# The B product of eight states as pairs in two row groups of the array, and the C product and sum of eight others in four column groups

## Chip, cores and metric

One core of one Trainium2 chip. The metric is the time of one execution on the device in microseconds; lower is better. Before the change three runs took 13143.59, 13146.60 and 13146.84 us, median 13146.6. All data is float32.

## What is computed

Two layers with a residual each. Layer 0 is a two-dimensional recurrence over a 64 x 64 image of 128 channels, 16 images. Layer 1, which the change touches, normalises its input in groups of channels and runs a selective state-space scan (Mamba) over the 4096 tokens of an image, once forwards and once backwards, with the same weights. Cut to layer 1, for one direction, with 256 inner channels d and 16 states s:

```python
xz = x @ in_w.T
xc, z = jnp.split(xz, 2, axis=-1)
xt = lax.conv_general_dilated(xt, conv_w[:, None, :], ..., feature_group_count=D_INNER)
xc = jax.nn.silu(jnp.transpose(xt, (0, 2, 1)))
dbl = xc @ x_w.T
dt, Bm, Cm = jnp.split(dbl, [DT_RANK, DT_RANK + D_STATE], axis=-1)
dt = jax.nn.softplus(dt @ dt_w.T + dt_b)
dA = jnp.exp(dt[..., None] * A)
dBx = dt[..., None] * Bm[:, :, None, :] * xc[..., None]
def step(h, inp):
    dA_t, dBx_t, C_t = inp
    h = dA_t * h + dBx_t
    y = jnp.einsum('bds,bs->bd', h, C_t)
    return (h, y)
y = jnp.swapaxes(ys, 0, 1) + xc * D
y = y * jax.nn.silu(z)
return y @ out_w.T
```

So for each of 16 states there is a decay exp(dt A), a drive dt x B (B is one number per token and state), a scan over the tokens, a product with C (again one number per token and state), and a sum over the states.

## The kernel before

Layer 0 comes first and takes about 1,560 us of the profiled execution. Layer 1 then makes 256 passes: 16 images, in each eight chunks of 512 tokens forwards and the same eight backwards. Channels lie on the 128 partitions in NH = 2 halves h, tokens along the free dimension; NB = 4 blocks j of 128 tokens make a chunk.

A pass does the following. PE convolves as eight products with shifted input (conv), ACT applies silu, PE makes dt, B and C (xproj, which already runs as two groups of 64 columns of the array), ACT copies them out, and they go to DRAM as 32 rows of 512 (rows). dtproj and softplus give dt; POOL multiplies dt and xc (times, giving dtx); PE turns dtx to have tokens on the partitions (turn), and ACT copies it (turn_take, giving dtxt). Then the states. For each, ACT makes the decay of the two halves (decay), DVE scans each half (scan, L1230), the last column is kept for the next chunk (keep, into carry), the state is multiplied by C (out_of; the row of C was spread over the partitions by a DMA of 256 KB, cr), and PE adds the turned product into the PSUM tile py (sums, eight turning matmuls). After all states, skip adds xc D, and finish takes py out; a forwards pass puts it in DRAM, a backwards pass adds it back (again), multiplies by the gate, turns it (back), projects it and stores it.

A string of letters, KINDS, says for each of the 16 states how its drive and its output are made:

- P: POOL multiplies dtx by the row of B spread over the partitions (drive, L1185); the decay lies in PSUM.
- M and T: ACT multiplies the turned dtx by B, a scalar per partition there, in four instructions (drive_turned, L1192); PE turns it back into PSUM (drive_back, L1218).
- N and U: PE turns back and multiplies at once, as a product with a diagonal matrix of B (drive_back, L1209). The diagonals dg are put together in DRAM by a DMA of single words onto a zeroed matrix (scatter, L1202), and loaded (spread).
- T and U scan in place in PSUM, and DVE makes their product with C (L1258); for all other letters POOL makes it (L1256).

Forwards passes have five M, four P, four N, two T, one U; backwards passes six M, five P, two N, two T, one U. In all that is 4.5 drives and 13 products with C on POOL a pass.

The order of all work on every engine is fixed when the program is built: order_of_issue lists the operations with costs (COST), priorities (URGENCY) and ring buffers (RINGS), and simulate places them, engine by engine, in an order. PSUM has eight banks: two for py, six handed out one by one, of which at most two at a time for "misc" (conv, xproj, dtproj, turn, gate, back, project) and at most five for decays and drives. The DMAs named here are all issued by SP, in order, and a DMA that must wait holds up those behind it. Softplus, silu and exp need different tables on ACT, so silu and softplus of passes ahead are gathered in a "session", with no decay between.

Of the kernel before, what the change touches and what calls it, by code (L numbers as in the profile page):

```python
# [14 lines left out]
P = 128  # L15
# [21 lines left out]
KINDS = ("MPNTMNPMUNPTMNPM", "MPMTPNMPTMPUMNPM")  # L37

RINGS = {
    "bank": 6, "py": 1, "das": 4, "dbx": 4, "dbt": 3, "dg": 3, "hst": 4, "hc": 5,  # L40
    "br": 4, "cr": 5, "xc": 2, "dt": 2, "dtx": 2, "dtxt": 2, "dbl": 2, "bt": 2, "z": 1, "y": 1,
    "yt": 1, "xr": 1, "xl": 1, "yo": 1, "yl": 1,
# [3 lines left out]
    "conv": 0.865, "gate": 0.87, "silu": 0.62, "softplus": 0.65, "gate_take": 0.6, "dtproj": 0.95,  # L46
    "xproj": 1.0, "xproj_take": 0.4, "bturn": 0.25, "bturn_take": 0.15, "times": 2.34,
    "turn": 0.47, "turn_take": 0.47, "decay": 0.62, "drive": 2.34, "drive_turned": 1.6,
    "drive_back": 0.44, "drive_back_diag": 0.88, "scan": 1.18,
    "keep_turned": 0.13, "keep": 0.6, "out_turned": 0.6, "out": 2.34, "sums": 0.88, "skip": 0.44,  # L50
# [7 lines left out]
LIMIT = {"misc": 2, "bank": 5}  # L58
AHEAD = 3
# [5 lines left out]
        {(0, 0): -27.9, (0, 1): -55.24, (0, 2): -37.14, (0, 3): -26.5, (1, 0): -25.66, (1, 1): -31.09,  # L65
         (1, 2): -28.23, (1, 3): -24.41},
        {(0, 0): -34.48, (0, 1): -62.91, (0, 2): -27.86, (0, 3): -25.86, (1, 0): -33.52, (1, 1): -26.55,
         (1, 2): -34.72, (1, 3): -27.13},
    ),
    "xproj": (  # L70
        {(): -7.14},
        {(): 5},
    ),
    "xproj_take": (
        {(): -0.87},
        {(): -6.61},
    ),
    "rows": (
        {(): 6.65},
        {(): 22.72},  # L80
    ),
    "bturn": (
        {(): -69.81},
        {(): -79.06},
    ),
    "bturn_take": (
        {(): -11.43},
        {(): -18.91},
    ),
    "dtproj": (  # L90
        {(0,): -63.21, (1,): -27.76},
        {(0,): -42.3, (1,): -15.88},
    ),
    "times": (
        {(): -134.9},
        {(): -152.1},
    ),
    "turn": (
        {(0,): -117.7, (1,): -95.41},
        {(0,): -92.29, (1,): -73.14},  # L100
    ),
    "turn_take": (
        {(0,): -12.62, (1,): -21.64},
        {(0,): -15.32, (1,): -17.24},
    ),
    "decay": (
        {(0, 0): 1.62, (0, 1): -12.81, (1, 0): -13.82, (1, 1): -8.37, (2, 0): 9.59, (2, 1): 7.54,
         (3, 0): -3.93, (3, 1): -3.12, (4, 0): -25.4, (4, 1): 2.96, (5, 0): 16.41, (5, 1): 14.98,
         (6, 0): -14.89, (6, 1): -7.22, (7, 0): 17.61, (7, 1): 6.71, (8, 0): -49.21, (8, 1): -31.38,
         (9, 0): 30.2, (9, 1): 28.66, (10, 0): -15.29, (10, 1): -11.14, (11, 0): -39.1, (11, 1): -52.04,  # L110
         (12, 0): 11.3, (12, 1): 12.04, (13, 0): -4.72, (13, 1): -9.28, (14, 0): -8.46, (14, 1): 9.15,
         (15, 0): 6.51, (15, 1): 10.38},
        {(0, 0): -11.72, (0, 1): -13.95, (1, 0): -23.83, (1, 1): -23.36, (2, 0): 5.39, (2, 1): 3.65,
         (3, 0): -27.89, (3, 1): -33.87, (4, 0): -17.63, (4, 1): -10.29, (5, 0): -5.06, (5, 1): 8.98,
         (6, 0): -5.94, (6, 1): 4.1, (7, 0): 5.44, (7, 1): 12.02, (8, 0): -73.78, (8, 1): -77.71,
         (9, 0): 21.8, (9, 1): 10.89, (10, 0): -3.99, (10, 1): -15.28, (11, 0): -27.37, (11, 1): -37.65,
         (12, 0): 21.39, (12, 1): 9.09, (13, 0): -2.78, (13, 1): -3.97, (14, 0): -1.99, (14, 1): 19.81,
         (15, 0): 11.27, (15, 1): 19.92},
    ),
    "spread": (  # L120
        {("c", 0): -1.78, ("c", 1): -117.27, ("b", 1): -23.09, ("c", 2): -80.12, ("d", 2): -40.37,
         ("c", 3): -18.07, ("c", 4): -0.55, ("c", 5): -99.41, ("d", 5): -52.16, ("c", 6): -133.17,
         ("b", 6): -13.49, ("c", 7): -18.83, ("c", 8): -39.5, ("d", 8): 9.08, ("c", 9): -42.09,
         ("d", 9): -26.61, ("c", 10): -81.5, ("b", 10): -14.43, ("c", 11): -35.04, ("c", 12): -76.62,
         ("c", 13): -69.54, ("d", 13): 21.06, ("c", 14): -21.91, ("b", 14): -26.12, ("c", 15): -95.57},
        {("c", 0): -14.51, ("c", 1): -135.28, ("b", 1): -22.37, ("c", 2): -75.2, ("c", 3): 26.76,
         ("c", 4): -11.36, ("b", 4): -10.82, ("c", 5): -37.95, ("d", 5): 9.47, ("c", 6): -122.31,
         ("c", 7): -91.31, ("b", 7): -6.34, ("c", 8): -1.04, ("c", 9): -15.62, ("c", 10): -118.12,
         ("b", 10): -20.57, ("c", 11): -6.63, ("d", 11): 42.13, ("c", 12): -104.85, ("c", 13): -62.16,
         ("d", 13): 36.52, ("c", 14): -56.98, ("b", 14): -28.81, ("c", 15): -80.03},  # L130
    ),
    "drive_turned": (
        {(0,): 4.39, (3,): 8.43, (4,): -6.7, (7,): -0.75, (11,): 7.02, (12,): -6.99, (15,): -17.26},
        {(0,): -1.81, (2,): -23.9, (3,): -35.33, (6,): -11.17, (8,): -20.91, (9,): -60.49, (12,): 7.71,
         (15,): 0.83},
    ),
    "drive_back": (
        {(0, 0): 3.71, (0, 1): 1.89, (2, 0): -5.19, (2, 1): -6.19, (3, 0): -4.81, (3, 1): 0.01,
         (4, 0): -2.71, (4, 1): 0.38, (5, 0): -18.47, (5, 1): 5.45, (7, 0): 9.18, (7, 1): 10, (8, 0): 9.85,
         (8, 1): 10.09, (9, 0): 10.62, (9, 1): 10.75, (11, 0): 3.53, (11, 1): 12.69, (12, 0): 4.21,  # L140
         (12, 1): 14.29, (13, 0): 12.99, (13, 1): 14.53, (15, 0): 16.89, (15, 1): 17.89},
        {(0, 0): -2.14, (0, 1): -4.49, (2, 0): -12.32, (2, 1): 4.91, (3, 0): -12.93, (3, 1): -0.55,
         (5, 0): -12.51, (5, 1): -4.37, (6, 0): -3.25, (6, 1): -2.4, (8, 0): 4.69, (8, 1): -1.16,
         (9, 0): 7.45, (9, 1): 9.75, (11, 0): 10.55, (11, 1): 10.75, (12, 0): 11.8, (12, 1): 14.97,
         (13, 0): 16.19, (13, 1): 16.9, (15, 0): 18.18, (15, 1): 10.8},
    ),
    "scan": (
        {(0, 0): 70.25, (0, 1): 59.47, (1, 0): 8.22, (1, 1): 9.32, (2, 0): -9.21, (2, 1): -2.84,
         (3, 0): 51.28, (3, 1): 75.32, (4, 0): 55.73, (4, 1): 59.47, (5, 0): 137.02, (5, 1): 138.28,
         (6, 0): 27.09, (6, 1): 15.69, (7, 0): 32.24, (7, 1): 37.07, (8, 0): 94.24, (8, 1): 108.17,  # L150
         (9, 0): 0.44, (9, 1): 28.19, (10, 0): 73.98, (10, 1): 59.24, (11, 0): 106.87, (11, 1): 94.54,
         (12, 0): -14.38, (12, 1): 5.54, (13, 0): 148.93, (13, 1): 161.13, (14, 0): 96.47, (14, 1): 100.3,
         (15, 0): 3.43, (15, 1): -30.56},
# [38 lines left out]
    ),  # L192
    "skip": (
        {(0,): -68.58, (1,): -75.02, (2,): -55.13, (3,): -52.01},
        {(0,): -75.1, (1,): -65.37, (2,): -44.94, (3,): -60.81},
    ),
    "finish": (
        {(): -74.82},
# [1203 lines left out]
```

## Time and profile before

| what | value |
|---|---|
| median of three runs | 13146.6 us |
| span of the profiled execution | 13233.8 us |
| starts of dtx, first and last of 256 | 1581.8 and 13159.4 us |
| scans, mean | 1261 ns, 32 a pass |
| products on POOL, mean | 2374 ns, 18.5 a pass |
| decays on ACT, mean | 713 ns into SBUF, 683 ns into PSUM |
| table loads on ACT, mean | 1283 ns, about 3 a pass |
| DMA of layer 1 | 0.63 to 0.65 of 16 engines busy, 165 GB/s |

The profile's columns: an engine's busy time counts overlapping instructions once, the mean is that of single instructions. PE's matmuls follow each other before the one ahead has ended, so a mean of 274 ns goes with a start every 109. "PEld" is the loading of the stationary matrix. A float32 product is two records of PE, a turning matmul one. In a group's line, behind the bar, stand its busy time, the mean duration in ns, and the idle time of the engine just before these instructions with what ended most of it. A line of the timeline gives the start in us, the duration of a merged run of equal instructions, engine, line and count.

### The profile page before, as it was taken

What the parts mean: (1) busy time and instruction counts of PE and PEld (TensorE: products, weight loads), DVE (VectorE), ACT (ScalarE), POOL (GpSimd) and SP (SyncE); (2) the same over time, 40 slices, a digit from 0 to 9 for tenths busy, and PEclk for the clock granted to TensorE, in tenths of its full rate; (3) what the DMA queues carried; (4) which work ended last, traced back from release to release, by engine and by line L of the source; (5) the groups of instructions that cost most, each with busy time, mean ns of one, the idle gap of its engine ahead of it and who ended that gap; (6) DMA issues with size and microseconds to landing.
All of it is one profiled execution on the core that took longest, in us unless ns stands there. A gap on an engine that the chain in (4) does not pass through costs nothing. (4 is left out here: it accounts for less than half of the span.)

```text
span 13233.8 us, 263820 instructions
## 1 busy us (share of the span) xinstructions
PE 12901.2 (97%) x91444; PEld 10833.0 (82%) x91444; DVE 12067.0 (91%) x14353; ACT 11513.4 (87%) x21184; POOL 11261.4 (85%) x4996
## 2 busy tenths in 40 slices
PE   8999999999999999999999999999999999999999
PEld 7666788888888888888888888888888888888887
DVE  6776699999999999999999999999999999999998
ACT  3444599999999999999999999999999999999998
POOL 0111299999999999999999999999999999999998
PEclk8999999999999999999999999999999999999999
DMA  4222265656666666656566666666665656666665
GB/s 143 54 57 54 63 172 158 172 156 172 161 167 165 164 165 160 172 158 172 158 170 161 166 165 163 166 159 172 158 173 160 169 162 168 164 163 166 163 166 145
DMA packets 2777751, 2025.28 MB, mean 153 GB/s; under 512 B 1584848, under 2 KB 1930464, under 8 KB 2776416
## 3 DMA queue, kind: packets, MB, share of 16 engines
q1 hardware_dynamic: 2698464, 1973.16, 57.5%
q10 hardware_dynamic: 77952, 35.24, 1.1%
q8 instruction: 725, 11.88, 0.4%
q14 instruction: 610, 5.00, 0.1%
HBM read 1849.24 MB, written 157.02 MB: 152 GB/s over the span
## 5 line engine op out<-in xcount | busy, mean ns | idle before, releaser
L1256 POOL TENSOR_TENSOR hc<-hst,cr 128x1024 f32<-128x1024 f32 x3328 | 7800.2, 2374 | 327.7 <-DVE hst L1230 243.2
L1230 DVE TENSOR_TENSOR_SCAN hst<-das,carry,hps 128x512 f32<-128x512 f32 x3808 | 4668.3, 1261 | 190.3 <-PE hps L1218 93.8
L1265 PE MATMUL py<-ident,hc 128*128 128x128 f32 x32768 | 4150.1, 274 | 57.2 <-POOL hc L1256 56.5
L1265 PEld LDWEIGHTS py<-ident,hc 128*128 128x128 f32 x32768 | 3676.6, 141 | 451.7 <-issue 272.5
L1180 ACT ACTIVATE das<-dt,A_log_sb 128x512 f32<-128x512 f32 x5888 | 3875.9, 713 | 121.5 <-DVE hst L1230 79.2
L1192 ACT ACTIVATE dbt<-dtxt,bt 128x256 f32<-128x256 f32 x7680 | 3231.7, 498 | 159.0 <-PE hps L1218 146.9
L1185 POOL TENSOR_TENSOR dbx<-dtx,br 128x1024 f32<-128x1024 f32 x1152 | 2724.6, 2378 | 10.1
L1230 DVE TENSOR_TENSOR_SCAN hst<-da,carry,dbx 128x512 f32<-128x512 f32 x2016 | 2468.8, 1260 | 31.7 <-ACT da L1180 30.0
L1218 PE MATMUL hps<-ident,dbt 128*128 128x128 f32 x15360 | 2264.2, 274 | 133.8 <-DVE hc L1258 109.3
L1209 PE MATMUL hps<-dg,dtxt 128*128 128x128 f32 x16384 | 2175.2, 277 | 38.7 <-DVE hst L1230 20.2
L1218 PEld LDWEIGHTS hps<-ident,dbt 128*128 128x128 f32 x15360 | 1783.9, 141 | 463.6 <-issue 329.7
L1209 PEld LDWEIGHTS hps<-dg,dtxt 128*128 128x128 f32 x16384 | 2004.6, 192 | 119.1 <-DVE hst L1230 45.9
L1049 PE MATMUL pp<-xT,wk 128*128 128x512 f32 x4096 | 1900.9, 596 | 0.5 <-DVE xl L837 0.5
L1230 DVE TENSOR_TENSOR_SCAN hps<-das,carry,hps 128x512 f32<-128x512 f32 x1344 | 1654.3, 1265 | 20.3 <-PE hps L1209 10.6
L1180 ACT ACTIVATE da<-dt,A_log_sb 128x512 f32<-128x512 f32 x2304 | 1556.2, 683 | 79.7 <-DVE hst L1230 58.6
L816 POOL TENSOR_TENSOR a_f<-a_f,c 128x288 f32<-128x288 f32 (+40 forms) x254 | 211.6, 833 | 1341.2 <-ACT a_f L808 1274.0
L1258 DVE TENSOR_TENSOR hc<-hps,cr 128x512 f32<-128x512 f32 x1536 | 1025.2, 674 | 258.5 <-DMA cr<-rows 247.7
L1049 PEld LDWEIGHTS pp<-xT,wk 128*128 128x128 f32 x4096 | 716.5, 190 | 627.7 <-issue 605.3
L1154 POOL TENSOR_TENSOR dtx<-dt,xc 128x1024 f32<-128x1024 f32 x256 | 607.9, 2374 | 280.4 <-ACT dt L1148 275.5
L1230 DVE TENSOR_TENSOR_SCAN hst<-das,hps 128x512 f32<-128x512 f32 x544 | 641.6, 1203 | 82.8 <-issue 27.1
L808 ACT ACTIVATE a_f<-pg_f,b_sb 128x288 f32<-128x288 f32 (+40 forms) x508 | 217.3, 471 | 361.9 <-DMA x<-xl 161.5
L1137 PE MATMUL pv<-dbl,dt_wT 128*128 128x256 f32 x2048 | 507.2, 380 | 8.5 <-ACT xc L1060 8.5
(115 smaller groups left out, 12672.9 us busy)
## 6 DMA issues: line engine op xcount, KB each, us to landing
cr<-rows SPq DMA_DIRECT2D x4096, 256.0 KB
br<-rows SPq DMA_DIRECT2D x1152, 256.0 KB
dg<-diag SPq DMA_DIRECT2D x1024, 256.0 KB
yf<-yo SPq DMA_DIRECT2D x128, 512.0 KB
yl<-yf SPq DMA_DIRECT2D x128, 512.0 KB
carry<-hst SPq DMA_DIRECT2D x3328, 1.0 KB
xs<-in_x_dram SPq DMA_DIRECT2D x64, 512.0 KB
xr<-x SPq DMA_DIRECT2D x128, 256.0 KB
```

Of the source, the lines that this page charges most:

```text
L1049: nc.tensor.matmul(self.ps["conv", h], lhsT=wk[:, k, h * P : (h + 1) * P], rhs=xT[self.b % 2][:, t0 : t0 + T], start=(k == 0), stop=(k == ...
L1137: nc.tensor.matmul(pv[:, q * TQ : (q + 1) * TQ], lhsT=dt_wT[:, q, h * P : (h + 1) * P], rhs=self.dbl, start=True, stop=True,)
L1154: nc.gpsimd.tensor_mul(self.dtx, self.dt, self.xc)
L1180: nc.scalar.activation(t, self.dt[:, h, :], AF.Exp, scale=amat[:, h, s : s + 1])
L1185: nc.gpsimd.tensor_mul(t, self.dtx, bc(self.brow.pop(s), 1, NH))
L1192: nc.scalar.activation(t[:, j, :], self.dtxt[:, j, :], AF.Copy, scale=self.bt[:, j, s : s + 1])
L1209: nc.tensor.matmul(t[:, j * P : (j + 1) * P], lhsT=self.dtxt[:, j, h * P : (h + 1) * P], rhs=self.dbt[s][:, j, :], start=True, stop=True,)
L1218: nc.tensor.transpose(t[:, j * P : (j + 1) * P], self.dbt[s][:, j, h * P : (h + 1) * P], ident)
L1230: nc.vector.tensor_tensor_scan(t[:, self.rev], self.da.pop((s, h))[:, self.rev], dbx[:, self.rev], 0.0 if self.first else carry[:, self.d, ...
L1256: nc.gpsimd.tensor_mul(self.hc[s], self.hst[s], bc(self.crow[s], 1, NH))
L1258: nc.vector.tensor_mul(self.hc[s][:, h, :], self.h[s, h], self.crow[s])
L1265: nc.tensor.matmul(self.py[:, j, cols], start=j not in self.banks, stop=last, skip_group_check=True, **how,)
```

## The change

All passes get the same string of two letters, eight states each:

- R: two states form a pair. PE makes the drives of both for one half in one operation, drive_rows. The turned dtx is now turned with a stride, so that partition i of block j holds token 4 i + j; partitions 0 to 63 then hold the first half of the chunk and 64 to 127 the second. For each j, two matmuls of 64 rows each run in the two row groups, each with a moving matrix of 128 columns (64 tokens by two states) into its own PSUM bank of a neighbouring pair. A scan reads every second word of that pair of banks. POOL makes the product with C, and sums adds it, as before.
- X: four states form a group, kept in one tile with the state as the innermost dimension, so that one state is every fourth word. POOL makes the drive into it, the scan runs in place (the decay is in PSUM), one DMA keeps the last columns of all four. Then PE turns the group, 32 tokens by four states at a time (turned, 16 a pass with four matmuls each), ACT copies it out (turned_take, 16 a pass), and weigh multiplies by a matrix of C and sums over the four states at once: for each block of 128 tokens four matmuls of 32 columns each, one per column group, add into 32 partitions of py each.

The matrices of both are put together in DRAM by scatter: for a pair two DMAs of 16-byte pieces, for a group one DMA of single words. drive_turned, bturn and the products with C on DVE go. dtproj becomes four matmuls of 64 rows in two row groups, in two banks that one softplus reads. The six PSUM banks become one tile with six parts. The session is placed behind all scans of the pass before. COST, RINGS and URGENCY have new values. The diff, cut:

```diff
-KINDS = ("MPNTMNPMUNPTMNPM", "MPMTPNMPTMPUMNPM")
+GX = 4
+TB = P // GX
+KINDS = ("XRRXXRRXXRRXXRRX", "XRRXXRRXXRRXXRRX")
...
-    "bank": 6, "py": 1, "das": 4, "dbx": 4, "dbt": 3, "dg": 3, "hst": 4, "hc": 5,
+    "bank": 6, "py": 1, "das": 3, "dg": 3, "group": 2, "cd": 2, "ht": 6, "hst": 3, "hc": 4, "dbx": 1,
...
+                after += [get(("scan", i - 1, s, h)) for s in range(NS) for h in range(NH)]
...
+            for jj in range(NB // 2):
+                ht = []
+                for k in range(4 * jj, 4 * jj + 4):
+                    b_, t = tile_of("misc"), tile_of("ht")
+                    ht.append(t)
+                    put("turned", (g, k), "PE", after=scans, takes=[b_], uses=[group], chain=("turned", 0))
+                    put("turned_take", (g, k), "ACT", after=[get(("turned", i, g, k))], takes=[t],
+                        uses=[b_], chain=("turned_take", 0))
+                put("weigh", (g, jj), "PE", after=[get(("turned_take", i, g, k)) for k in range(4 * jj, 4 * jj + 4)]
+                    + [landed, get(("finish", i - 1))] + skips, uses=ht + [cd])
...
+        banks = psum.tile([P, RINGS["bank"], T], F32, name="banks")
...
+            def dtproj(self, *places):
+
+                low, high = places = sorted(places)
+                self.ps["dt"] = banks[:, low : high + 1 : high - low, :]
+                for h in range(NH):
+                    for q in range(NQ):
+                        rows = slice(q * QP, (q + 1) * QP)
+                        nc.tensor.matmul(
+                            banks[:, places[q], h * TQ : (h + 1) * TQ],
+                            lhsT=dt_wT[rows, h * P : (h + 1) * P],
+                            rhs=self.dbl[rows, :],
...
             def turn(self, i, place):
 
-                pt = self.ps["turn", i] = bank(place, f"ptx_{self.nm}_{i}", (P, 2, DI))
+                pt = self.ps["turn", i] = bank(place, (P, 2, DI))
+                strided = self.dtx.rearrange("p h (i j) -> p h j i", j=NB)
                 for j in range(2):
                     for h in range(NH):
                         nc.tensor.transpose(
-                            pt[:, j, h * P : (h + 1) * P],
-                            self.dtx[:, h, (2 * i + j) * P : (2 * i + j + 1) * P],
-                            ident,
+                            pt[:, j, h * P : (h + 1) * P], strided[:, h, 2 * i + j, :], ident
                         )
...
             def drive(self, s):
-                t = ring(sp, "dbx", [P, NH, T], f"dbx_{self.nm}_{s}")
+                kind, st, g, m = self.plan[s]
+                if kind == "P":
+                    t = ring(sp, "dbx", [P, NH, T], f"dbx_{self.nm}_{s}")
+                else:
+                    if m == 0:
+                        self.group[g] = ring(sp, "group", [P, NH, T, GX], f"group_{self.nm}_{g}")
+                    t = self.group[g][:, :, :, m]
                 nc.gpsimd.tensor_mul(t, self.dtx, bc(self.brow.pop(s), 1, NH))
...
+            def scatter(self, kind, g):
+
+                t = diags[self.number % SETS][kind, g]
+                if kind == "d":
+                    st = next(p[1] for p in self.plan if p[0] == "R" and p[2] == g)
+                    step = P // NQ
+                    for k in range(2):
+                        dst = bass.AP(
+                            t.tensor, t.offset + k * NB, [[T + 2 * NB, step], [step * T, NQ], [1, NB]]
+                        )
...
+                st = NS + g * GX
+                dst = bass.AP(t.tensor, t.offset, [[GX * T + 1, TB], [T, GX], [TB, T // TB]])
...
+            def drive_rows(self, s, h, *places):
+
+                low, high = sorted(places)
+                g = self.plan[s][2]
+                step = P // NQ
+                dg = self.mat["d", g].rearrange("p (i n j) -> p j i n", n=2, j=NB)
+                pair = banks[:, low : high + 1, :].rearrange("p r t -> p (r t)")
                 for j in range(NB):
+                    for r in range(NQ):
+                        rows = slice(r * step, (r + 1) * step)
+                        half = banks[:, low + r, :].rearrange("p (i j n) -> p j i n", j=NB, n=2)
                         nc.tensor.matmul(
+                            half[:, j, :, :],
+                            lhsT=self.dtxt[rows, j, h * P : (h + 1) * P],
+                            rhs=dg[rows, j, :, :],
...
+                for k in range(2):
+                    self.dbx[s + k, h] = pair[:, k::2]
...
+            def turned(self, g, k, place):
+
+                pt = self.ps["turned", g, k] = bank(place, (P, 2, DI))
+                for j in range(2):
                     for h in range(NH):
+                        t0 = (2 * k + j) * TB
+                        nc.tensor.transpose(
+                            pt[:, j, h * P : (h + 1) * P], self.group[g][:, h, t0 : t0 + TB, :].rearrange("p t s -> p (t s)"), ident
                         )
+
+            def turned_take(self, g, k):
+                t = self.ht[g, k] = ring(sp, "ht", [P, 2, DI], f"ht_{self.nm}_{g}_{k}")
+                nc.scalar.copy(t, self.ps.pop(("turned", g, k)))
+
+            def weigh(self, g, jj):
+
+                cd = self.mat["k", g].rearrange("p (k t) -> p k t", t=TB)
+                for j in range(2 * jj, 2 * jj + 2):
+                    for q in range(GX):
+                        k = GX * j + q
+                        nc.tensor.matmul(
+                            self.py[q * TB : (q + 1) * TB, j // 2, (j % 2) * DI : (j % 2 + 1) * DI],
+                            lhsT=cd[:, k, :],
+                            rhs=self.ht[g, k // 2][:, k % 2, :],
+                            start=False,
```

## Prediction

> **What bounds the kernel now.** I read the page's busy table first, then stretches of exactly one image, then the groups, then the timeline around the one place where the array is already split.
>
> ```profile
> span 13233.8 us, 263820 instructions
> ...
> PE 12901.2 (97%) x91444; PEld 10833.0 (82%) x91444; DVE 12067.0 (91%) x14353; ACT 11513.4 (87%) x21184; POOL 11261.4 (85%) x4996
> ```
>
> The first 1,560 us or so belong to layer 0, which the change leaves alone. Of layer 1, two stretches of one image (16 passes) each, busy time in the order PE, weight load, DVE, ACT, POOL, then granted clock and DMA share:
>
> ```profile
> 2400.00:3123.00 723.00, 707.97 (x5254) 605.63 (x5253) 684.60 (x729) 675.56 (x1222) 686.84 (x296) 1.00 0.64 165
> 3123.00:3846.00 723.00, 709.08 (x5264) 606.78 (x5264) 685.53 (x731) 676.51 (x1224) 687.50 (x295) 1.00 0.63 165
> ```
>
> PE is busy 98%, DVE and POOL 95%, ACT 94%, at full clock: nothing has slack, and PE has least. The waits are small and scattered, and the chain that ended last holds only the last 25 us. So the time is the sum of work on the fullest engine plus a little. The starts of the product dtx, one a pass, give the period: 45.40 us a pass over all 256; over 15 images the eight first-direction passes average 43.55 us and the eight second-direction ones 47.3 us.
>
> Prices come from these groups (count, busy us, mean ns) and from distances between starts in the trace:
>
> ```profile
> L1256 POOL TENSOR_TENSOR hc<-hst,cr 128x1024 f32<-128x1024 f32 x3328 | 7800.2, 2374 | 327.7 <-DVE hst L1230 243.2
> L1230 DVE TENSOR_TENSOR_SCAN hst<-das,carry,hps 128x512 f32<-128x512 f32 x3808 | 4668.3, 1261 | 190.3 <-PE hps L1218 93.8
> L1265 PE MATMUL py<-ident,hc 128*128 128x128 f32 x32768 | 4150.1, 274 | 57.2 <-POOL hc L1256 56.5
> ...
> L1192 ACT ACTIVATE dbt<-dtxt,bt 128x256 f32<-128x256 f32 x7680 | 3231.7, 498 | 159.0 <-PE hps L1218 146.9
> ...
> L1218 PE MATMUL hps<-ident,dbt 128*128 128x128 f32 x15360 | 2264.2, 274 | 133.8 <-DVE hc L1258 109.3
> L1209 PE MATMUL hps<-dg,dtxt 128*128 128x128 f32 x16384 | 2175.2, 277 | 38.7 <-DVE hst L1230 20.2
> ```
>
> The means overlap, so a stream costs its start distance: a turning matmul 0.109 us, a true product 0.112 (128 columns), 0.216 (256), 0.430 (512); each true product counts as two records. A POOL product costs 2.325, a scan 1.171, a copy of 128x512 on ACT 0.466, a quarter of drive_turned 0.399.
>
> **The price of a split array** is already in the trace, because xproj runs as two column groups:
>
> ```profile
> 6006.92 0.60 PE L1218 MATMUL hps<-ident,dbt 128*128 128x128 f32 x4
> 6007.45 1.08 PE L1087 MATMUL pd<-xc,x_wT_sb 128*64 128x256 f32 x8
> 6008.47 1.60 PE L1265 MATMUL py<-ddiag,xc 128*128 128x128 f32 x12
> ...
> 6023.62 1.03 PE L1137 MATMUL pv<-dbl,dt_wT 128*128 128x256 f32 x4
> ```
>
> Eight matmuls of 256 columns end in 1.08 us where four unsplit ones need 1.03: pairs start 7 ns apart and run wholly side by side. But entry and exit cost. Medians over 256 passes: the first matmul starts 94 ns late, the four pairs span 705 ns instead of 654, the next instruction starts 310 ns after the last instead of 216, the one after it 165 instead of 110. Together 0.295 us per excursion into the split array and back.
>
> **The change on PE, per pass** (first direction / second direction / mean). Removed: half of the sums, 64 x 0.109 = 6.98; the turning back of seven / eight states, 6.1 / 6.98, mean 6.54; the products with a diagonal of five / three states, 8.96 / 5.38, mean 7.17; bturn 0.22; the full-height dtproj 1.73. Mean 22.64. Added: 16 turned, 64 x 0.109 = 6.98; eight drive_rows of eight pairs, 8 x (8 x 0.112 + 0.295) = 9.53; four weigh of four quadruples, 4 x (4 x 0.216 + 0.295) = 4.64; dtproj 4 x 0.216 + 0.295 = 1.16. Together 22.31. The untouched rest is 18.1 / 23.8 (half the sums, conv, xproj, turn, skip, read; in the second direction gate, again, back, project). PE goes from 42.07 / 45.06 to 40.4 / 46.1: almost level, cheaper in one direction and dearer in the other. The gain of packing is nearly eaten by 13 excursions a pass, 3.8 us. Two halves of one drive_rows pair need the same matrix, so I let two of the 13 join a neighbour: 39.8 / 45.5.
>
> No row splits the array by rows, or into four. Bounds for drive_rows: wholly side by side 1.19, in turn 16 x 0.112 + 0.295 = 2.09 us. For weigh: four abreast 1.16, two abreast 2.02. I take side by side, the nearest row being xproj; the other ends go to the rivals.
>
> The Trainium skill speaks against drive_rows here ("TensorE: Matmul & The Clock Gate", "LDWEIGHTS (loading the stationary operand)"): a load's time follows its columns and not its rows. Two half-height loads of 128 columns would each take the time of a full one, and by its columns/1.2 ns (an estimate, 107 ns) sixteen in turn would make the sum 2.0 us instead of 1.19; xproj's 64-column loads cannot show which holds, though they started 6 ns apart.
>
> **POOL**: drives 4.5 to 8, products with C 13 to 8, dtx 1: 18.5 to 17 products, 43.0 to 39.5 us; with the 1.2 us that it waits for dt before each dtx in the first direction, 40.7. **DVE**: six products with C (0.583) and six carry copies (0.063) go, -3.9 us; scans stay at 32. **ACT**: 30 quarters of drive_turned go (-12.0) and bturn_take (-0.09), 16 copies come (+7.5): -4.6. These gains are worth nothing while PE is the fullest; they hide under it.
>
> **Strides.** The X states live four to a group, so drive writes, and the scan reads and writes, every fourth word; no scan or POOL row has that. One DVE row does:
>
> ```profile
> L834 DVE TENSOR_TENSOR xl<-ph,xl 128x256 f32<-128x256 f32 x16 | 6.8, 424 | 2.8 <-DMA xl<-in_x_dram 1.7 <-PE ph L831 0.9
> ...
> L928 DVE TENSOR_TENSOR wk<-in_wT,xT 128x256 f32<-128x256 f32 x4 | 2.4, 604 | 0.0
> ```
>
> L928 reads one operand at every fourth word and takes 180 ns more on 256 elements, 0.70 ns each. Bounds: nothing, or 0.70 ns on every element, which is +0.72 us per drive (POOL 45.3) and +0.36 per X scan (DVE from 38.9 to 44.7). I take nothing: L928's 604 ns over 256 are 2.36 ns an element at most, a scan already spends 1171/512 = 2.29 and a POOL product 2.27, so a slower access fits almost wholly inside. The same goes for the strided reads of drive_rows' matrix and of turn, where the bound is inside the 2.09 above and 0.9 us for turn. Its results go to PSUM in pairs of words; no row has that, and the same two ends hold.
>
> The skill ("GPSIMD Engine Reference", "Performance pitfalls for Q7 kernels") gives about one more cycle an element for reads with steps above 8 bytes. If it held for the writes too, a drive would cost 0.85 us more (an estimate at 1.2 GHz) and POOL 46.3; no row before shows a strided POOL operand.
>
> **DMA and queues.** Rows and matrices of 256 KB: 24.5 a pass to 22. Scatters: four issues to ten, keeps 13 to 10. SP spends 24.2 us a pass issuing; now 22 x 0.39 + 10 x 0.61 + 8 x 0.59 + two large scatters at 0.59 to 2.4 each (512 elements cost 0.59; these have 2048) + 2 = 23 to 26 us. Cost nothing, under the 40 us and more of the engines; uncovered, a late matrix stops PE. 4-byte packets took 9 ns each; some 2,300 more small ones a pass are 1.3 us of the 16 engines, and the large ones fall by more. On ACT the session (silu two passes ahead, softplus) is now placed after all scans of the pass before; behind it the decays queue, and DVE waits for them; covered by the 4.6 us that ACT gains, bare it is two table loads and four activations, some 5 us.
>
> **Sum.** First direction: PE 39.8, POOL 40.7; above the greater I keep 1.2 of the 1.48 us that the period now stands above PE: 41.9. Second: 45.5 + 1.4 of the present 2.24, as POOL no longer competes: 46.9. Against 43.55 and 47.3 that is 2.05 us less for a pair of passes, 128 x 2.05 = 262 us: the profiled execution goes from 13,234 to 12,972. That execution lies 87 us above the median shown, so 13,146.6 - 262 = **12,885 us**. With no joins and the old slack: 42.2 and 48.3, 0.3 us less the pair, 13,100; with half of the excursions joined (-1.9) and 1 us of slack, 41.7 and 45.2: 12,640. Its own range is 12,450 to 13,110.
>
> **Rivals.**
> Drive_rows in turn (loads or strided reads): +8 x 0.90 = 7.2 us on PE, 47.6 / 53.3, with 2% idle 48.5 / 54.3, so 13,147 + 128 x 11.95 = 14,680. For it: loads of 128 columns are recorded at 192 ns and xproj's at 137, and nothing in the trace loads two halves of 128 at once. Against: the pairs of xproj. It decides the sign once a drive_rows costs about 1.3 us, as 8 x 0.13 eats the 1.03 us a pass.
> Buffers: sixteen turned a pass go through the two banks kept for such work, which conv also holds until its silu; a group buffer is kept from its first drive to its last turning, two buffers for two groups a pass. If that idles PE 2.5 us a pass: 44.4 / 49.4, 13,147 + 128 x 2.95 = 13,520. For it: a turn, hand-over and copy take about 1.3 us at the least, 21 us of two banks shared. Against: ACT has 4.6 us less to do.
> Strided POOL writes at L928's price: POOL 45.3 in both directions, with its wait 46.5, in the second beside a PE of 45.5 some 47.5: 13,147 + 128 x 3.15 = 13,550.
> Weigh two abreast: 4 x 0.86 = 3.4 on PE, periods of 44.4 / 50.3, 13,640; nothing in the trace has four.
> The change does not do what it says on balance: excursions take all that packing gives, 13,147.
>
> **How the numbers follow.** Forecast 0.50; in turn 0.12; buffers 0.17; POOL 0.10; weigh 0.06; no change 0.05. Faster 0.50, same 0.05, slower 0.45; 0.2% is about what a measurement of this kernel can tell. The range 12,450 to 13,900 leaves out the first rival and a little at the low end.
>
> **What would show it.** Right: eight pairs of drive_rows in about 1.2 us with starts a few ns apart, weigh in 1.2, strided drives at 2.37 and X scans at 1.26, POOL down to some 90% of a first-direction pass. Wrong: drive_rows spanning 2 us, drives near 3.1, PE idle before turned or weigh waiting for ACT, DVE waiting for a drive that waits for a group buffer.

## Result and profile after

| kernel | device time, us | against before, 95% interval |
|---|---|---|
| before | 13,145 (13,138 to 13,147) | 1 |
| changed | 35,627 (35,623 to 35,648) | 2.711 (2.707 to 2.715) |

The change makes the kernel 2.7 times slower, where 12,885 us was forecast. The page of the changed kernel, its head and the row of the granted clock:

```profile
span 35625.6 us, 290279 instructions
...
PE 21843.7 (61%) x108340; PEld 14423.4 (40%) x108340; DVE 11756.9 (33%) x11281; ACT 11074.4 (31%) x17344; POOL 10390.6 (29%) x4612
...
PEclk9866666666666666666666666666666666666666
```

GpSimd has as much less to do as the sum said (POOL 11,261 to 10,391), VectorE and ScalarE about a third of what it said (DVE 12,067 to 11,757 where 1,000 less were forecast, ACT 11,513 to 11,074 where 1,180 were), and yet no engine is busy more than 61% of the span. So this is no engine that became too full: they wait. The granted clock of PE is 0.65 in the mean: the trace has it at full for 10,600 us and at half for 25,000. The groups:

```profile
L1346 POOL TENSOR_TENSOR hc<-hst,cr 128x1024 f32<-128x1024 f32 x2048 | 4802.1, 2353 | 19125.2 <-DVE hst L1322 12229.1
L1322 DVE TENSOR_TENSOR_SCAN group<-banks,carry,group 128x512 f32<-128x512 f32 x3584 | 4584.0, 1282 | 10174.1 <-ACT ht L1360 2826.1
L1322 DVE TENSOR_TENSOR_SCAN hst<-das,carry,banks 128x512 f32<-128x512 f32 x3584 | 4553.6, 1278 | 9500.2 <-ACT ht L1360 1585.9
...
L1302 PE MATMUL banks<-d,dtxt 64*128 64x128 f32 x32768 | 4377.7, 420 | 3223.0 <-ACT banks L1252 1166.1
...
L1263 POOL TENSOR_TENSOR group<-dtx,br 128x1024 f32<-128x1024 f32 x2048 | 4832.4, 2382 | 4567.7 <-PE banks L1354 2040.1
```

The single instructions are nearly as fast as forecast: the drive at every fourth word 2,382 ns (2,374 to 2,378 before), scans 1,278 and 1,282 ns (1,261 before). What is new stands behind the bar. L1322's scans, which read decays and drives, wait for `ACT ht L1360`, the copy of a turned block, with which they have no data in common. The timeline shows how (start and duration in us; in brackets the idle time before it and what ended it):

```profile
16039.38 0.66 PE L1354 MATMUL banks<-ident,group 128*128 128x128 f32 x4 [0.83 <-ACT ht L1360]
16040.13 1.28 DVE L1322 TENSOR_TENSOR_SCAN hst<-das,carry,banks 128x512 f32<-128x512 f32 x1 [1.97 <-PE banks L1354]
...
16041.47 2.07 PE L1302 MATMUL banks<-d,dtxt 64*128 64x128 f32 x16 [1.43 <-DVE hst L1322]
...
16043.58 0.58 ACT L1360 COPY ht<-banks 128x512 f32<-128x512 f32 x1 [3.64 <-PE banks L1302]
...
16044.26 1.28 DVE L1322 TENSOR_TENSOR_SCAN hst<-das,carry,banks 128x512 f32<-128x512 f32 x1 [2.84 <-ACT ht L1360]
...
16045.68 1.10 PE L1234 MATMUL banks<-ident,dtx 128*128 128x128 f32 x4 [2.15 <-DVE hst L1322]
...
16046.82 0.69 ACT L1252 ACTIVATE banks<-dt,A_log_sb 128x512 f32<-128x512 f32 x1 [2.03 <-PE banks L1234]
```

Read it downwards: PE turns a block into one bank, done at 16040.04. Next DVE scans a pair of other banks. Only then does PE make a drive in a third place, only then does ACT copy the block that has lain ready for 3.5 us, only then comes the scan of the drive, and so on. PE, DVE and ACT take turns at PSUM, one operation each, whichever bank it touches. Six banks are there for three engines to use at once, and one engine at a time uses them.

### The profile page after: what moved, and what is told of

It is laid out like the page before. It is cut to its first block, busy times and chain, and to the rows that moved or that the text cites. A ratio compares the mean times of both kernels' runs of the same rounds, so it can differ in the third digit from the quotient of the medians.

```text
span 35625.6 us, 290279 instructions
## 1 busy us (share of the span) xinstructions
PE 21843.7 (61%) x108340; PEld 14423.4 (40%) x108340; DVE 11756.9 (33%) x11281; ACT 11074.4 (31%) x17344; POOL 10390.6 (29%) x4612
## 5 line engine op out<-in xcount | busy, mean ns | idle before, releaser
L1346 POOL TENSOR_TENSOR hc<-hst,cr 128x1024 f32<-128x1024 f32 x2048 | 4802.1, 2353 | 19125.2 <-DVE hst L1322 12229.1
L1322 DVE TENSOR_TENSOR_SCAN group<-banks,carry,group 128x512 f32<-128x512 f32 x3584 | 4584.0, 1282 | 10174.1 <-ACT ht L1360 2826.1
L1322 DVE TENSOR_TENSOR_SCAN hst<-das,carry,banks 128x512 f32<-128x512 f32 x3584 | 4553.6, 1278 | 9500.2 <-ACT ht L1360 1585.9
L1354 PE MATMUL banks<-ident,group 128*128 128x128 f32 x16384 | 3837.8, 386 | 4950.8 <-ACT banks L1252 1361.3
L1302 PE MATMUL banks<-d,dtxt 64*128 64x128 f32 x32768 | 4377.7, 420 | 3223.0 <-ACT banks L1252 1166.1
L1252 ACT ACTIVATE banks<-dt,A_log_sb 128x512 f32<-128x512 f32 x4096 | 2832.4, 692 | 11158.1 <-DVE hst L1322 3027.9
L1263 POOL TENSOR_TENSOR group<-dtx,br 128x1024 f32<-128x1024 f32 x2048 | 4832.4, 2382 | 4567.7 <-PE banks L1354 2040.1
L1302 PEld LDWEIGHTS banks<-d,dtxt 64*128 64x128 f32 x32768 | 3648.7, 280 | 4393.0 <-ACT banks L1252 1423.5
L1354 PEld LDWEIGHTS banks<-ident,group 128*128 128x128 f32 x16384 | 2644.4, 195 | 6292.7 <-ACT banks L1252 1769.9
L1127 PE MATMUL banks<-xT,wk 128*128 128x512 f32 x4096 | 3584.1, 985 | 2580.2 <-DVE group L1322 1071.7
L1360 ACT COPY ht<-banks 128x512 f32<-128x512 f32 x4096 | 2336.1, 586 | 6506.2 <-PE banks L1354 2945.1
L1322 DVE TENSOR_TENSOR_SCAN group<-banks,group 128x512 f32<-128x512 f32 x512 | 625.9, 1223 | 1429.0 <-ACT ht L1360 498.3
L1322 DVE TENSOR_TENSOR_SCAN hst<-das,banks 128x512 f32<-128x512 f32 x512 | 622.2, 1219 | 1419.9 <-ACT banks L1252 300.2
```

The source lines that it names most:

```text
L1127: nc.tensor.matmul(self.ps["conv", h], lhsT=wk[:, k, h * P : (h + 1) * P], rhs=xT[self.b % 2][:, t0 : t0 + T], start=(k == 0), stop=(k == ...
L1252: nc.scalar.activation(t, self.dt[:, h, :], AF.Exp, scale=amat[:, h, st : st + 1])
L1263: nc.gpsimd.tensor_mul(t, self.dtx, bc(self.brow.pop(s), 1, NH))
L1302: nc.tensor.matmul(half[:, j, :, :], lhsT=self.dtxt[rows, j, h * P : (h + 1) * P], rhs=dg[rows, j, :, :], start=True, stop=True, skip_grou ...
L1322: nc.vector.tensor_tensor_scan(t[:, self.rev], self.da.pop((s, h))[:, self.rev], dbx[:, self.rev], 0.0 if self.first else carry[:, self.d, ...
L1346: nc.gpsimd.tensor_mul(self.hc[s], self.hst[s], bc(self.crow[s], 1, NH))
```

## Experiments

Each run stands beside runs of the kernel before on the same chip, whose medians were 13,227 to 13,239 us there. Runs 4, 8, 9 and 12 were timed four times, the others once.

**1. One tile for six banks, in the kernel before.**

```diff
-            return psum.tile(list(shape), F32, name=name, tag=f"bank{place}")
+            t = banks[: shape[0], place, : T if len(shape) == 2 else None]
...
+        banks = psum.tile([P, RINGS["bank"], T], F32, name="banks")
```

> The kernel before, with one edit: its six PSUM banks are one tile with six parts, as in the changed kernel; everything else, the order of the work too, is as before. Theory (the one tile makes TensorE, VectorE and ScalarE take turns, whichever bank each of them touches): between 25,000 and 40,000 us, the granted clock well below 0.97, and scans that wait for copies out of banks that they do not read. Rival one (the new matmuls in row and column groups and the data at a stride of four are what is slow): 13,150 us, no change. Rival two (the new order of work and its buffers): 13,150 us as well.

31,226 us, as the theory had it. This edit alone, with every instruction of the engines and their order as in the kernel before, costs 18,000 us. Its page and some of its timeline:

```profile
span 31224.6 us, 264227 instructions
...
PE 20069.4 (64%) x91444; PEld 14827.9 (47%) x91444; DVE 12935.9 (41%) x14353; ACT 11823.0 (38%) x21184; POOL 11306.9 (36%) x4996
```

```profile
16001.05 1.02 PE L1053 MATMUL banks<-xT,wk 128*128 128x512 f32 x2
...
16002.16 1.28 DVE L1234 TENSOR_TENSOR_SCAN hst<-banks,carry,dbx 128x512 f32<-128x512 f32 x1 [1.67 <-PE banks L1053]
...
16003.50 1.13 PE L1053 MATMUL banks<-xT,wk 128*128 128x512 f32 x2 [1.43 <-DVE hst L1234]
...
16004.66 1.28 DVE L1234 TENSOR_TENSOR_SCAN hst<-banks,carry,dbx 128x512 f32<-128x512 f32 x1 [1.22 <-PE banks L1053]
```

The convolution is cut into pieces: a scan waits for a part of it, the next part for the scan. The same 91,444 matmul records that took PE 12,901 us take 20,069, at a granted clock of 0.73.

**2 and 3. Three tiles of two banks, in both kernels.**

```diff
+        banks = [psum.tile([P, 2, T], F32, name=f"banks{i}") for i in range(RINGS["bank"] // 2)]
...
-                pair = banks[:, low : high + 1, :].rearrange("p r t -> p (r t)")
+                pair = banks[low // 2].rearrange("p r t -> p (r t)")
```

> The kernel before with its six PSUM banks as three tiles of two banks. Theory: only the two banks of a tile hold each other up, so clearly above 13,150 and far below the one-tile version: 13,800 to 20,000 us. Rivals one and two: 13,150 us.

> The changed kernel with its six banks as three tiles of two banks (the pairs of states always lie in banks 2k and 2k+1, so a pair still fits one tile); softplus takes the two halves of dt in two activations of 256 columns, since they can lie in different tiles. Theory: most of the loss comes back, 14,000 to 21,000 us, with the clock up. Rival one (the new matmuls and strides): above 30,000 us. Rival two (order and buffers): above 25,000 us.

15,753 and 17,417 us, both in the theory's ranges and outside the rivals'. The more banks share a tile, the more is lost: 13,235, 15,753 and 31,226 us for the kernel before with one, two and six banks to a tile.

**4. Six tiles of one bank in the changed kernel.**

```diff
-        banks = psum.tile([P, RINGS["bank"], T], F32, name="banks")
+        banks = [psum.tile([P, T], F32, name=f"bank{i}") for i in range(RINGS["bank"])]
...
-                    self.dbx[s + k, h] = pair[:, k::2]
+                    self.dbx[s + k, h] = [banks[low + r][:, k::2] for r in range(NQ)]
...
+                for cols, drive in parts:
+                    nc.vector.tensor_tensor_scan(t[:, cols][:, self.rev], da[:, cols][:, self.rev], drive[:, self.rev], start, ...)
+                    edge = cols.start if self.d else cols.stop - 1
+                    start = t[:, edge : edge + 1]
```

> The changed kernel with six tiles of one bank each. A state of a pair is then scanned in two chained scans of 256 columns, one in each bank (16 scans more in a pass), and softplus takes two activations instead of one. Theory: all of the loss comes back but what the rest of the change costs; by the sum of the prediction 12,900 us plus the 16 more scans, 12,800 to 14,300 us. Rival one: above 30,000 us. Rival two: 15,000 to 30,000 us, with waits for group buffers and turned blocks at the top of the list of waits.

15,588 us, 1.178 of before (1.176 to 1.180). Of the 22,480 us that the change lost, 20,040 are back (the kernel before differs by 0.7% between the two chips). The expectation of at most 14,300 was missed, so there is a second loss. The time lies in the range of rival two, the order of work and the buffers, but waiting is not the main part of it: PE is busy 95% of the span and idles 733 us, 333 before. Page and groups of drive_rows:

```profile
span 15550.2 us, 293005 instructions
...
PE 14817.3 (95%) x108340; PEld 10950.5 (70%) x108340; DVE 11984.9 (77%) x15377; ACT 10599.7 (68%) x17856; POOL 10463.9 (67%) x4612
...
L1302 PE MATMUL bank<-d,dtxt 64*128 64x128 f32 x32768 | 4341.5, 410 | 129.7 <-DVE hst L1329 39.1
L1302 PEld LDWEIGHTS bank<-d,dtxt 64*128 64x128 f32 x32768 | 3353.3, 201 | 912.8 <-issue 301.2
```

Now PE is full again, with 1,916 us more work than before, where the prediction had about 85 less without joined excursions. There are 2,048 drive_rows (eight a pass), so 4,341.5 us are 2.12 us each where 1.19 was taken, excursion included. Starts tell more: the two records of a pair start 7 or 8 ns apart, so the row groups do run side by side, but pair follows pair only every 227 ns. (The 218 ns of the expectations, and the 105 to 110 hoped for there, count from the second record of a pair to the first of the next. A "matmul" of 109 ns there is one record; a float32 product is two.)

**5 to 8. What makes a pair slow.** My first theory was the loading of weights: two half-height loads of 128 columns for every pair.

```diff
-                            lhsT=self.dtxt[rows, j, h * P : (h + 1) * P],
+                            lhsT=self.dtxt[rows, j, h * P : h * P + P // 2],
```

> The changed kernel with six tiles of one bank, where each matmul of drive_rows loads only the first 64 of its 128 weight columns (the B product of channels 64 to 127 and 192 to 255 is left out; their scans read what the bank held). In the six-tile kernel two row groups start 7 to 10 ns apart, but a pair takes 218 ns and 16 matmuls 2.06 us, where the prediction had 1.19. Theory (the pair is bound by its two weight loads of 128 columns, 204 ns each side by side): a pair falls to about 110 ns, 16 matmuls to 1.1 to 1.3 us, and the time from 15,590 to 13,700 to 14,300 us. Rival one (the moving data are streamed in turn, or at the strides of the diagonal and of the bank they are slow): a pair stays at 218 ns, 15,590 us.

```diff
-                            rhs=dg[rows, j, :, :],
+                            rhs=dg[rows, j, : P // 4, :],
```

> The same six-tile kernel, where each matmul of drive_rows keeps its 128 weight columns but moves only the first 64 of its 128 columns (the B product of the later half of each 256 steps is left out). Theory (weight loads): a pair stays at about 218 ns, 16 matmuls at 2.0 us, 15,400 to 15,600 us. Rival one (streaming): a pair at about 110 ns, 16 matmuls at 1.0 to 1.3 us, 13,700 to 14,300 us.

```diff
-                for j in range(NB):
-                    for r in range(NQ):
+                for r in range(NQ):
+                    for j in range(NB):
```

> The same six-tile kernel with the two loops of drive_rows exchanged: the four matmuls of the lower 64 rows first, then the four of the upper ones, so that no two neighbours can run side by side. Theory (weight loads set the time, one load of 128 columns after another): the time stays within 1% of 15,590 us. Rival one (the two row groups do share time, and would cost more in turn): 16 matmuls at 3 us or more, 17,000 to 18,500 us.

```diff
-                dg = self.mat["d", g].rearrange("p (i n j) -> p j i n", n=2, j=NB)
+                dg = self.mat["d", g].rearrange("p n (i j) -> p n j i", j=NB)
...
+                    strided = t.rearrange("p (i j) -> p j i", j=NB)
...
+                            lhsT=self.dtxt[:, j, h * P : (h + 1) * P],
+                            rhs=dg[:, k, j, :],
```

> The six-tile kernel with the B product of the pair taken on the whole array: for each of the two states a diagonal of its own, four matmuls of 128 rows by 128 columns into a bank of its own (the diagonals of a pair are two loads of 256 KB instead of one; two buffers for such pairs instead of three for one, and three buffers instead of four for the C rows, so that it fits). No excursion into the split array, and one scan of 512 columns for a state again. Theory: drive_rows at 8 matmuls of 0.112 us, 0.9 us instead of 2.06 plus 0.32 for the excursion; 2,048 times 1.4 us less than 15,590, so 12,700 to 13,300 us, about as the kernel before or under it. Rival two (order and buffers are what keeps it above): 14,000 us or more, with TensorE idle for over 10% of the span.

| run | time, us | busy of drive_rows / 2,048 |
|---|---|---|
| 4, six tiles | 15,588 | 2.12 us |
| 5, half the weights | 15,498 | 2.07 us |
| 6, half the moving columns | 14,789 | 1.25 us |
| 7, rows in turn | 17,365 | 2.93 us |
| 8, whole array | 18,208 (ratio 1.376, 1.374 to 1.378) | 3.80 us |

The theory of the loads fell: halving them shortens the median load from 204 to 151 ns and leaves a pair at 227. Halving the moving columns halves it, to 117 ns, though the time, 14,789, missed the 14,300 of that rival by 490; its page:

```profile
span 14787.2 us, 293005 instructions
...
PE 13410.3 (91%) x108340; PEld 9886.6 (67%) x108340; DVE 11948.6 (81%) x15377; ACT 10587.8 (72%) x17856; POOL 10443.7 (71%) x4612
```

Run 7 falls under its first rival: records of one row group follow each other every 227 ns, and a drive_rows costs 0.8 us more, though where the upper rows take over from the lower some records still start 6 ns apart. So the row groups share time. Run 8 pointed to the cause by missing worst. Its group:

```profile
L1298 PE MATMUL bank<-d,dtxt 128*128 128x128 f32 x32768 | 7781.9, 406 | 34.3 <-ACT ht L1359 24.3
```

That is the very shape of L1209 before (277 ns, a start every 112), but with 406 ns and a start every 227. What differs is that the columns of the diagonal and of the bank are 16 bytes apart; this run can't tell the two strides from each other.

**9 to 11. Which stride.**

```diff
-                dg = self.mat["d", g].rearrange("p (i n j) -> p j i n", n=2, j=NB)
+                dg = self.mat["d", g].rearrange("p (j i n) -> p j i n", n=2, j=NB)
```

> The six-tile kernel with the diagonals laid out so that the 128 moving columns of a matmul of drive_rows lie next to each other (columns ordered j, i, n; before i, n, j, that is a stride of 16 bytes); the bank is still written at strides. The scatter then moves single elements, in twice as many DMAs. The halved moving columns brought a pair from 218 to 110 ns, half the weights brought nothing, and on the whole array at stride four a matmul took 227 ns where the kernel before has 112 for the same shape without strides: one of the two strides halves the rate at which columns go through. Theory one (the moving operand's stride): a pair at about 110 ns, 16 matmuls at 1.0 to 1.2 us, 13,300 to 13,900 us. Theory two (the stride of what is written into the bank): unchanged, 15,500 to 15,700 us.

```diff
-                        half = banks[low + r].rearrange("p (i j n) -> p j i n", j=NB, n=2)
+                        half = banks[low + r].rearrange("p (j i n) -> p j i n", j=NB, n=2)
```

> The six-tile kernel where drive_rows reads its moving columns at the old stride but writes them next to each other in the bank (columns ordered j, i, n, so that the steps of time stand in another order and the scans compute something else). Theory one (the moving operand's stride): unchanged, 15,500 to 15,700 us. Theory two (the bank's stride): 13,300 to 13,900 us, a pair at about 110 ns.

> Both edits of the two runs beside it: neither the moving columns nor the bank's at a stride (the order of time in the bank is changed, as there). Both theories: a pair at about 110 ns and 13,300 to 13,900 us; if it takes both strides away to get there, only this one does.

15,907 (1.203, 1.201 to 1.205), 15,571 and 15,933 us. Run 10 does what theory one said; the times of runs 9 and 11 miss under either theory, and the groups decide. Run 9, then run 10:

```profile
L1303 PE MATMUL bank<-d,dtxt 64*128 64x128 f32 x32768 | 2580.2, 291 | 477.7 <-DVE hst L1330 378.3
```

```profile
L1302 PE MATMUL bank<-d,dtxt 64*128 64x128 f32 x32768 | 4340.2, 410 | 127.5 <-DVE hst L1329 38.5
```

With the moving columns in one run a drive_rows is busy 2,580.2 / 2,048 = 1.26 us and pairs start 112 ns apart, no more than one record on the whole array took in L1209 before; with the bank's columns in one run nothing changes (2.12 us, 227 ns). Theory one holds for the cost of the operation.

The trace of the changed kernel says the same in another way. Where the granted clock is at half, a record of sums starts every 213 ns, and 109 at full; a pair of drive_rows starts every 228 ns at half and 227 at full. With its columns in one run (run 9) a pair goes from 112 to 214. So at the step of 16 bytes the clock of PE is not what limits a pair.

Run 9 is slower than run 4 all the same, for another reason. A wait in run 9 (us in total, times, longest), then the same in run 4:

```profile
DVE hst L1330 <- DMA carry<-hst: 1102.8, 270, 10.4
```

```profile
DVE hst L1329 <- DMA carry<-hst: 103.8, 76, 3.7
```

The scatter now moves single words in twice as many DMAs, and the scans wait for carries, which are queued with it on SP.

**12. The same, without the small transfers.**

```diff
+                nc.scalar.copy(
+                    t.rearrange("p j (i n) -> p j i n", n=2),
+                    self.mat["d", g].rearrange("p (i n j) -> p j i n", n=2, j=NB),
+                )
...
-                            rhs=dg[rows, j, :, :],
+                            rhs=dg[rows, j, :],
```

> The six-tile kernel with drive_rows' moving matrix in one run, as in the run with the scatter of single elements, but made another way: scatter keeps its 16-byte pieces, and ScalarE copies each loaded matrix once into the other order (four copies of 128x512 a pass, about 0.7 us each; two buffers for loaded and two for copied matrices, three for the C rows). Theory (the moving operand's stride is what drive_rows lost, and the other version's gain on TensorE was given back by its small transfers in front of the carries on SP's queue): a pair at 105 to 110 ns, 14,600 to 15,100 us, as the run with half the moving columns, and no wait of a scan for a carry near the top. Rival one (the order of the work and its buffers do not let the time fall below 15,500 whatever drive_rows costs): 15,500 to 15,900 us. Rival two (all that the six-tile kernel still lost was drive_rows): 12,900 to 13,500 us.

15,137 us, 1.144 of before (1.142 to 1.146): the best of the changed kernels that leave nothing out, 450 us under run 4, just above the range given, and still behind the kernel before. To make room the run also keeps three buffers instead of four for the rows of C, and two instead of three for the loaded matrices. Page and waits:

```profile
span 15134.2 us, 293108 instructions
...
PE 13327.4 (88%) x108340; PEld 9849.0 (65%) x108340; DVE 11955.1 (79%) x15377; ACT 11613.2 (77%) x18880; POOL 10447.1 (69%) x4612
...
L1313 PE MATMUL bank<-de,dtxt 64*128 64x128 f32 x32768 | 2518.2, 289 | 609.8 <-ACT de L1296 419.6
...
L1296 ACT COPY de<-d 128x512 f32<-128x512 f32 x1024 | 1170.8, 1143 | 109.4 <-DMA d<-d 109.4
```

```profile
PE py L1402 <- POOL hc L1368: 545.3, 281, 5.6
PE bank L1313 <- ACT de L1296: 419.6, 254, 7.1
...
POOL hc L1368 <- DMA cr<-rows: 232.4, 97, 10.1
DVE hst L1342 <- DMA carry<-hst: 218.9, 161, 4.5
```

The wait for carries is down to 219 us, and drive_rows is at 1.23 us. PE has 1,490 us less to do than in run 4, but idles 1,807 us instead of 733 (span less busy): 1,074 of the 1,490 are given back as waiting. Some 420 of that is the new copy, which at 1,143 ns is slower than I took it for; another 350 is PE waiting for products of POOL (545 us, 194 in run 4). These wait for scans most of all (1,607 us), and now also for rows of C (232 us, 22 in run 4), which may be the price of the buffer given up. Rival two of this run, that drive_rows was all that run 4 still lost, falls, and so does rival one, that nothing would take the time below 15,500.

## Why the prediction was wrong

**The step that failed is one that the sum does not contain.** The text before the prediction states that the six PSUM banks become one tile with six parts; the prediction gives it no price and no rival. Runs 1 to 4 price it: 18,000 us in the kernel before, 20,040 of the 22,480 us in the changed one. Between run 4 and the changed kernel the 108,340 matmul records are the same; PE's idle time goes from 733 to 13,782 us and its busy time from 14,817 to 21,844, at a granted clock of 0.65 instead of 0.99: of the 20,075 us between the two spans, 13,050 are waiting and 7,030 are slower work. The chip does not ask for those waits, as runs 1 and 4 show on the same banks. They come with the program: what different engines do with one PSUM tile is kept in order, and by these runs a tile of several banks is kept in order as a whole. (The kernel before takes a new tile for each use of a bank; run 4 keeps six for good, as the changed kernel keeps its one, so keeping a tile is not what costs.) The list of changes had to be read for that too: a renaming of storage moves no work, but it can add waits to every instruction that touches it. "What would show it" looked for waits at buffers and banks of the new operations; the sign to look for was an engine that waits for an instruction with which it shares no data.

**Drive_rows at 1.19 us.** Wrong by 0.93: 2.12, or 8 x 0.93 x 256 = 1,900 us of PE's work, and by the prediction's own sum this alone would have made the change slower. The rival "in turn (loads or strided reads)" had the size, 2.09, and its second reason was right, not the first, and not the words "in turn": pairs do run side by side, but the moving matrix is read at 16-byte steps, and that halves the rate of its columns (227 ns a pair, 112 without). The working did name the strided read and bounded it inside the 2.09, and took nothing, since slow elements of DVE and POOL could hide a slower access. That argument did not carry to PE, which takes a column every 0.88 ns (112 ns for 128). With the columns in one run a drive_rows is busy 1.23 to 1.26 us, so "side by side", the forecast's choice against its rival, was right.

**The rule on loads.** The rule drawn from the Trainium skill ("TensorE: Matmul & The Clock Gate", "LDWEIGHTS (loading the stationary operand)"), that loads would price drive_rows at 2.0, came near the number for a reason that the runs refute: in run 9 two half-height loads of 128 columns go by every 112 ns. What the page states agrees with the runs: a load of 128 columns is recorded at 201 ns with 64 rows (run 4) and 192 with 128 (before), one of 64 columns at 147 (run 5). What failed is that the loads of the two row groups would go in turn. A rule that bears on it stands elsewhere in the skill: "Advanced Engine Details and Errata", "SBUF Cachelines", says that accesses which each go to another 16-byte line are penalised. Runs 4 and 9 agree, with 227 against 112 ns a pair, and run 8 is in line, with 227 against 112 a record. Its neighbour "PSUM Cachelines" has it that any non-contiguous pattern in PSUM slows matmuls, and that every two consecutive elements should be contiguous; runs 9 and 11, 1.26 us both, agree with the second and show no cost where only pairs of words are contiguous.

**What was right.** Strides cost POOL next to nothing: a drive took 2,382 ns (run 4: 2,404) for 2,370 forecast. X scans took 1,282 (run 4: 1,265) for 1,260. weigh runs four abreast: its quadruples start 217 ns apart in run 4 (the second 241 after the first), priced at 216, and going in and out of the split array costs it 94 and 94 ns, as xproj. dtproj's eight records end in 1.05 us. POOL has less to do by what was said (870 us for 900). In run 4 SP's queue and the carries cost next to nothing (104 us).

**Slack.** The sum kept 1.2 to 1.4 us a pass above PE. With PE within 600 us of the priced work (runs 6 and 12, 13,410 and 13,327 us for some 12,820), it idled 1,377 and 1,807 us of the span, 333 before. So with both failed steps mended, as these runs mend them, the forecast stayed out of reach: run 6, with half of the moving columns left out, took 14,789. Of the 1,900 us that the span of run 12 is above that of the kernel before, 426 are PE's work and 1,474 its waiting. Which of the order of issue, the buffers or the halved scans (which come with the six tiles and not with the change) makes PE wait there is open; no run took them apart. The rival "buffers" had its waits on turned blocks; in run 12 PE's largest waits are for POOL and for the copy instead.

## What to carry to other kernels

Before costing instructions, go through a change for storage that is merged, and ask of each pair of engines that touch it whether they now wait for each other; separate banks used by different engines belong in separate tiles, also where one access pattern over all of them would be handy. Keep the moving operand of a matmul in consecutive words: a step of 16 bytes doubled the time of every column, and that took all that packing two row groups had gained. And an engine relieved is not a span relieved: once the fullest engine gets less work, see which waits were hidden under it, as 1,074 of 1,490 us came back here.

## What the runs showed of the hardware

Two half-height loads of 128 columns and two streams of 128 columns go side by side every 112 ns (runs 9 and 12), the time of one full-height record before, so row groups do double the rate, loads included. With the moving columns 16 bytes apart a pair takes 227 ns, at the full granted clock and at half of it. A strided PSUM write (pairs of words 32 bytes apart) costs PE nothing (1.26 us for a drive_rows in runs 9 and 11), and a scan or a POOL product at every fourth word next to nothing (1,265 ns for 1,261, 2,404 for 2,378); but a copy on ACT that reads SBUF at steps of 16 bytes took 1,143 ns, where plain ones of 128x512, which read PSUM, take 590 and decays, which read SBUF, 726 (run 4). The granted clock sank to 0.65 with PE busy 61% of the span, though 10,900 of the 13,700 us that PE idled in layer 1 lay in gaps of 1 to 4 us. The busy share alone does not tell it: in run 7 PE was busy 97% at 0.952, in run 2 86% at 0.985.
